# A graph layer's edge sum: the transposed node table built in the prologue, and another split of the gathers between engines

## The chip, the cores and the metric

The kernel runs on 1 core of a Trainium2 chip. The metric is the device time of one execution in microseconds (us); the time before is the median of three runs.

## The reference

One message-passing layer over a graph with 12500 nodes of 48 features and 400000 edges that are sorted by their destination. A node's features are normalised and rectified; for each edge, a two-layer perceptron takes destination, source and the edge's own 32 features; the messages are summed by destination and added to the input.

```python
h = jnp.maximum(_layernorm(x, axis=-1), 0.0)
x_i = h[dst]; x_j = h[src]
tmp = jnp.concatenate([x_i, x_j, edge_attr], axis=1)      # 48 + 48 + 32
h2 = jax.nn.relu(tmp @ W1 + b1)                           # 128 wide
msg = h2 @ W2 + b2                                        # 48 wide
out = x + jax.ops.segment_sum(msg, dst, num_segments=12500)
```

## The kernel before

`tmp @ W1` is split into three products. Two of them depend on a node alone, so a prologue (`node_tables`) makes two tables in DRAM: `tab_a` (what a node contributes as destination, with the bias) and `tab_b` (what it contributes as source), a row of 128 floats a node. The prologue goes over the nodes in six slices: VectorE and ScalarE normalise, PE transposes a slice into `ht`, and `table` multiplies it with the weights, two groups of 128 nodes a matmul; ScalarE and VectorE copy PSUM into `tab`, SyncE writes it out. First all of `tab_b`, then all of `tab_a`.

The main part (`windows`) goes over the 400000 edges in 391 chunks of 8 tiles of 128 edges. The 80 nodes from a chunk's first destination on are its window. Per chunk:

- `prepare`: SyncE loads the window's 80 rows of `tab_a` (`rhs`), the edges' features into the lower rows of `lhs`, and the destinations (`row`). VectorE compares `row` with the window's numbers, which makes a one-hot matrix in the upper rows of `lhs` and the nodes' degrees (`deg`), and makes a second one-hot matrix `hot`, with the edges along the partitions.
- `before`: PE multiplies `lhs` and `rhs` into `pre` (PSUM): destination and edge part of the hidden layer.
- `hidden`: VectorE adds the source part `gb`, ScalarE rectifies: `hid`.
- `fold`, `add`: PE sums `hid` by window node through `hot` into `p_g`; VectorE adds it into the running accumulator `seg` at the place of the window. Every 12 chunks a group's accumulator goes through W2 and out (`segment_*`).

The source part, a row of `tab_b` for each edge, comes in one of three ways:

- *gathers*: POOL issues one indirect DMA for a tile of 128 edges into `gb`. There are six `gb` buffers of a chunk each, so POOL runs up to six chunks ahead, until `hid` has read the oldest.
- *columns*: the transposed `tab_b` also lies in SBUF, as `bt` (128 x 12544). VectorE and ScalarE copy one column of four bytes per partition for an edge into a tile `gt`; a PE matmul (`turned` in `windows`) adds it into `pre`. The node's number is loaded from `last` into a register of the copying engine (`load`, by `numbers`), up to 32 a load instruction.
- *rows*: SyncE issues a DMA of one row for an edge into a tile `gs`, with the number from a register.

104 columns (44 on VectorE, 60 on ScalarE) and 12 rows are made per chunk, whatever tile they belong to; `BYCOLS` and `BYROWS` list the chunks whose last tile is complete by then and is not gathered. `PARTS` gives each part's engine, first column, size, and place in `last`.

`bt` is made in the first 13 chunks: `turn_load` reads 1024 rows of `tab_b` back from DRAM, `turn` transposes them with eight PE transposes, ScalarE copies them out. Columns therefore begin with chunk 14.

The order on each engine is that of the program text (a manual schedule). An iteration c of the main loop is written as follows, where each engine takes its own part in this order:

```python
prepare(c); turn_load(c); rows(c)
columns(c, 0); columns(c, 1)               # VectorE
before(c - 1); fold(c - 2); turned(c - 1)  # PE
columns(c, 2); hidden(c - 1)
load(c, 3); columns(c, 3)                  # ScalarE
add(c - 2)
load(c + 1, 0); load(c + 1, 2); turn(c)
```

`load(c, 1)` stands in `prepare`, between VectorE's comparison and `hot`. `deg` and `seg` are cleared at the head of `windows`, in a pool that takes the SBUF space the prologue's tiles give back.

Of the kernel before, what the change touches and what calls it, by code (L numbers as in the profile page):

```python
# [8 lines left out]
F32 = mybir.dt.float32  # L9
I32 = mybir.dt.int32  # L10
AF = mybir.ActivationFunctionType
ALU = mybir.AluOpType
# [18 lines left out]
L = 1024  # L31
# [14 lines left out]

BUILD = (NPAD + CE - 1) // CE
COLS = BUILD + 1  # L50
ROWS0 = 3
END = NT // T

PARTS = ((True, 0, 27, 1), (True, 27, 17, 28), (False, 44, 28, 48), (False, 72, 32, 76))
PART = sum(n for _, _, n, _ in PARTS)
BASE = 108
RPART = 12

BT0 = 16512


SEG, NEXT, SEG2 = 122, 123, 124
WIDTH = 128
SLOTS = (NCH + 2 + P - 1) // P
MOST = 32

# [15 lines left out]
GNACC = 4  # L82


def node_tables(nc, tc, keep, x, ident, w1, b1, tab_a, tab_b, loads, most, check, rest):

    slices = [(0, 8), (8, 16), (24, 20), (44, 20), (64, 20), (84, 14)]
    ns = len(slices)
# [3 lines left out]
    with ExitStack() as es:  # L92
# [72 lines left out]
        def table(j, wt, tv, dve):  # L165
# [17 lines left out]
                    nc.scalar.copy(to, of)  # L183
            nc.sync.dma_start(tv[:, r0 : r0 + rb, :], t)

        for i in range(ns + 3):
            if i < ns:
                centre(i)
            if 0 <= i - 1 < ns:
                scale(i - 1)  # L190
            if 0 <= i - 2 < ns:
                turn(i - 2)
            if i == ns + 1:
                most()
            if i == ns + 2:
                check()
            if 0 <= i - 3 < ns:
                table(i - 3, wb, tb_v, i >= ns)
        for j in range(ns):
            table(j, wa, ta_v, True)  # L200
        rest()


def windows(nc, tc, gp, bt, ident, idx, x_t, tab_a, tab_b, dst, edge_t, w1, w2s, b2s, out_t):


    srci, rel, bw, wrow, last = idx
    with ExitStack() as es:
        one = es.enter_context(tc.tile_pool(name="wone", bufs=1))
        ld = es.enter_context(tc.tile_pool(name="ld", bufs=3))  # L210
        gtp = es.enter_context(tc.tile_pool(name="gtp", bufs=3))
# [13 lines left out]
        for _, _, n, at in PARTS:  # L225
# [4 lines left out]
        rows_at = slice(BASE + 1, BASE + 1 + RPART)  # L230
# [3 lines left out]
        tab8 = tab_b.rearrange("n h -> (n h)").bitcast(U8)  # L234

        place = PARTS[0][3] - 1
        for a, b in ((place, SEG2), (NEXT, SEG)):
# [5 lines left out]
        segs = []  # L243
        for k in range(2):
            seg = one.tile([P, 2, L], F32, name=f"seg{k}")
            nc.vector.memset(seg, 0.0)
            segs.append(seg)
        degs = []
        for k in range(3):
            deg = one.tile([W, P], F32, name=f"deg{k}")  # L250
            nc.gpsimd.memset(deg, 0.0)
            degs.append(deg)

        rhss = []
        for k in range(3):
# [7 lines left out]
        def group(c):  # L263

            return divmod(c + OFF, GQ)
# [15 lines left out]
        def node(n):  # L281
            return n.with_bounds(min_val=0, max_val=N - 1)
# [11 lines left out]
                    tab8[bass.ds(n, 4 * HID)].rearrange("(o h) -> o h", o=1),  # L294
                )

        def turn_load(i):

            n = min(T, NR - i * T)
            t = wp.tile([P, T, HID], F32, name="hid")  # L300
            nc.sync.dma_start(
                t[:, :n, :],
                tab_b[i * CE : i * CE + n * P, :].rearrange("(t p) h -> p t h", p=P),
            )
            return n, t

        def turn(i, n, t):
            p_t = ps_p.tile([P, T, HID], F32, name="pre")
            for q in range(n):
                nc.tensor.transpose(p_t[:, q, :], t[:, q, :], ident)  # L310
            nc.scalar.copy(  # L311
                bt[:, i * CE : i * CE + n * P], p_t[:, :n, :].rearrange("h t p -> h (t p)")
            )

        regs = {}

        def load(c, part):

            dve, first, n, at = PARTS[part]
            n = max(0, min(n, len(BYCOLS) * P - ((c - COLS) * PART + first))) if c >= COLS else 0  # L320
            engine = mybir.EngineType.DVE if dve else mybir.EngineType.Activation
            if part == 0 and 2 <= c < NCH + 2:
                base, *nodes = numbers(c, at - 1, n + 1, engine)
                st[c - 2]["base"] = base.with_bounds(min_val=0, max_val=FAR)
            else:
                nodes = numbers(c, at, n, engine) if n else []
            regs[c, part] = nodes

        def columns(c, part):

            dve, first, _, _ = PARTS[part]
            copy = nc.vector.tensor_copy if dve else nc.scalar.copy
            for k, at in enumerate(regs.pop((c, part), [])):
                j, e = divmod((c - COLS) * PART + first + k, P)
                of = BYCOLS[j]
                if of not in gts:
                    gts[of] = gtp.tile([HID, P], F32, name="gt")
                at = at.with_bounds(min_val=BT0, max_val=BT0 + 4 * (N - 1)) - BT0
                copy(gts[of].bitcast(U8)[:, 4 * e : 4 * e + 4], bt8[:, bass.ds(at, 4)])  # L339

        def prepare(c):
            n = min(T, NT - c * T)
            at = c * CE
            m = max(0, min(RPART, len(BYROWS) * P - (c - ROWS0) * RPART)) if c >= ROWS0 else 0
            base, *nodes = numbers(c, BASE, 1 + m, mybir.EngineType.SP)
            rhs = rhss[c % 3]
            nc.sync.dma_start(rhs[:W, :], tab_a[bass.ds(node(base), W), :])
            lhs = ld.tile([P, CE], F32, name="lhs")
            nc.sync.dma_start(lhs[W:K, : n * P], edge_t[:, at : at + n * P])
            row = ld.tile([W, CE], I16, name="row")  # L350
            nc.sync.dma_start(
                row[:, : n * P],
                dst[at : at + n * P].rearrange("(o e) -> o e", o=1).to_broadcast([W, n * P]),
            )
            st[c] = dict(n=n, rows=nodes)
            gb = gp.tile([P, T, HID], F32, name="gb")
            for t in range(n - (c in BYCOLS) - (c in BYROWS)):
                nc.gpsimd.indirect_dma_start(  # L358
                    out=gb[:, t, :], out_offset=None, in_=tab_b[:, :],
                    in_offset=bass.IndirectOffsetOnAxis(  # L360
                        ap=srci[:, c * T + t : c * T + t + 1], axis=0
                    ),
                )

            deg = degs[c % 3]
            nc.vector.tensor_scalar(  # L366
                lhs[:W, : n * P], row[:, : n * P], bw[:, c : c + 1], None,
                op0=ALU.is_equal, op1=ALU.add, accum_out=deg[:, :1],
            )
            load(c, 1)  # L370
            hot = wp.tile([P, T, W], F32, name="hot")
            nc.vector.tensor_tensor(  # L372
                hot[:, :n, :], wnum.unsqueeze(1).to_broadcast([P, n, W]),
                rel[:, c * T : c * T + n].unsqueeze(2).to_broadcast([P, n, W]), op=ALU.is_equal,
            )
            st[c].update(rhs=rhs, lhs=lhs, gb=gb, deg=deg, hot=hot)

        def before(c):
# [43 lines left out]
        def add(c):  # L422

            s = st.pop(c)
            to = segs[group(c)[0] % 2][:, :, bass.ds(s["base"], W)]
            nc.vector.tensor_add(to, to, s["p_g"])  # L426

        xs = {}
# [31 lines left out]
        with tc.manual_schedule():  # L460
            for c in range(NCH + 2):
                if c < NCH:
                    prepare(c)
                    if c < BUILD:
                        part = turn_load(c)
                    rows(c, st[c].pop("rows"))
                columns(c, 0)
# [29 lines left out]
                if c < BUILD:  # L497
# [131 lines left out]
def tile_gnn_preln(  # L629
# [51 lines left out]
    bw = const.tile([W, NCH], F32, name="bw")  # L681
    flag = const.tile([1, 1], I32, name="flag")
    last = const.tile([P, SLOTS, WIDTH], I32, name="last")
    gp = ctx.enter_context(tc.tile_pool(name="gp", bufs=6))

    with tc.tile_pool(name="keep", bufs=1) as keep, tc.tile_pool(
# [68 lines left out]

        dsts = keep.tile([P, NT], F32, name="dsts")
        b0f = keep.tile([P, NCH], F32, name="b0f")
        node_tables(nc, tc, keep, x, ident, w1, b1, tab_a, tab_b, loads, most, check, rest)
    outside = nc.values_load(flag[:1, :1], min_val=0, max_val=1)

    with tc.If(outside == 0) as cmp:
        windows(nc, tc, gp, bt, ident, (srci, rel, bw, wrow, last), x_t, tab_a, tab_b, dst16, edge_t,
                w1, w2s, b2s, out_t)
    with cmp.Else():
        general(nc, tc, bt, ident, x_t, tab_a, tab_b, src_it, dst_it, dst, edge_t, w1, w2s, b2s,
# [71 lines left out]
```

## Time and profile before

| what | value |
|---|---|
| three runs | 4942.31, 4946.85, 4949.29 us; median 4946.85 |
| profiled execution | 4948.09 us, its span 4946.4 us |
| first gather on POOL | 67.24 us |
| `seg` of the first chunk, `seg` of the 15th | 147.3 us, 324.4 us |
| POOL's gathers (L358) | 2784 |
| column copies (L339) on ScalarE, VectorE | 22500, 16540 |
| row transfers (L292) | 4608 |
| register loads (L274) on VectorE | 800, median 1410 ns |
| granted TensorE clock, mean | 0.607 |

The times of the trace count from the span's start. An engine counts as busy while it carries out an instruction of its own; register loads, semaphore waits and the issue of a DMA don't count, and "issue" stands for idle time in which the profile shows nothing that the engine waited for. "remote" stands for a wait whose releaser isn't among the instructions shown.

### The profile page before, as it was taken

How to read it: one execution, taken by the hardware profiler on the slowest of the kernel's cores; microseconds unless marked ns; L12 is line 12 of the kernel's file. 1: busy time of each engine (PE TensorE's matmuls, PEld its weight loads, DVE VectorE, ACT ScalarE, POOL GpSimd, SP SyncE). 2: the span in 40 equal slices, each digit the busy share in tenths (PEclk: the TensorE clock that was granted, in tenths of full speed). 3: DMA queues.
4: the chain of work that ended last, by engine and by line, in shares of the span. 5: the costliest groups of instructions: out<-in, count | busy, mean ns of one | idle time of the engine just before them, and what ended most of it. 6: DMA issues, size and time to landing. Idle time of an engine off the chain costs nothing. (4 is left out here: it accounts for less than half of the span.)

```text
span 4946.4 us, 92158 instructions
## 1 busy us (share of the span) xinstructions
PE 3197.2 (65%) x14504; PEld 2884.0 (58%) x14504; DVE 2942.6 (59%) x18764; ACT 2864.2 (58%) x23270; POOL 2675.9 (54%) x2812
## 2 busy tenths in 40 slices
PE   4565666666666666666666666666666666666666
PEld 3555556555555555656555555655666555555656
DVE  3255666666666666566666666666566666666665
ACT  2146666666566666566656566666566666566665
POOL 5555555555555555555555555555555555555552
PEclk7665655566666565556565666555555665666555
DMA  5422222222222222222222222222222222222221
GB/s 208 111 78 71 70 70 67 68 70 72 70 70 68 67 70 71 70 70 69 66 70 71 70 70 68 67 70 70 70 70 68 68 69 71 70 69 69 70 67 51
DMA packets 214695, 363.63 MB, mean 74 GB/s; under 512 B 70419, under 2 KB 119717, under 8 KB 212805
## 3 DMA queue, kind: packets, MB, share of 16 engines
q0 software_dynamic: 89120, 182.66, 14.4%
q1 hardware_dynamic: 124704, 174.89, 11.8%
q14 instruction: 491, 4.01, 0.3%
q8 instruction: 120, 1.97, 0.2%
q10 hardware_dynamic: 260, 0.10, 0.0%
HBM read 337.91 MB, written 22.07 MB: 73 GB/s over the span
## 5 line engine op out<-in xcount | busy, mean ns | idle before, releaser
L358 POOL DMA_INDIRECT gb<-tab_b,srci x2784 | 2654.2, 953 | 2167.6 <-DVE seg L426 1273.1
L339 ACT COPY gt<-bt 128x4 uint8 x22500 | 2421.0, 189 | 1761.1 <-issue 1734.7
L339 DVE COPY gt<-bt 128x4 uint8 x16540 | 1516.0, 193 | 1464.2 <-issue 1457.9
L416 PE MATMUL p_g<-hot,hid 128*128 128x80 f32 x6250 | 1368.2, 407 | 1557.6 <-ACT hid L408 1446.3
L416 PEld LDWEIGHTS p_g<-hot,hid 128*128 128x128 f32 x6250 | 1291.5, 314 | 1648.2 <-ACT hid L408 1528.5
L384 PEld LDWEIGHTS pre<-rhs,lhs 112*128 112x128 f32 x6250 | 1254.8, 306 | 140.1 <-issue 95.7
L384 PE MATMUL pre<-rhs,lhs 112*128 112x128 f32 x6250 | 1291.4, 393 | 52.1 <-DVE hid L403 38.8
L366 DVE TENSOR_SCALAR_CACHE_REDUCE lhs<-row,bw 80x1024 f32<-80x1024 int16 x391 | 498.1, 1274 | 253.5 <-issue 181.1
L403 DVE TENSOR_TENSOR hid<-pre,gb 128x896 f32<-128x896 f32 (+2 forms) x391 | 429.7, 1099 | 67.5 <-remote 53.8
L408 ACT ACTIVATE hid<-hid 128x896 f32<-128x896 f32 (+1 forms) x391 | 376.1, 962 | 120.4 <-DVE hid L403 91.1
L372 DVE TENSOR_TENSOR hot<-wnum,rel 128x640 f32<-128x640 f32 x391 | 322.0, 823 | 95.7 <-issue 95.7
L394 PE MATMUL pre<-ident,gt 128*128 128x128 f32 x610 | 220.0, 464 | 93.6 <-remote 49.8
L419 PE MATMUL p_g<-ident,deg 80*128 80x80 f32 x782 | 237.4, 405 | 2.7 <-issue 2.7
L394 PEld LDWEIGHTS pre<-ident,gt 128*128 128x128 f32 x610 | 164.0, 328 | 101.3 <-remote 53.6
L419 PEld LDWEIGHTS p_g<-ident,deg 80*128 80x128 f32 x782 | 203.4, 317 | 2.7 <-issue 2.7
L426 DVE TENSOR_TENSOR seg<-seg,p_g 128x160 f32 x391 | 120.9, 309 | 51.3 <-issue 23.4
L452 PE MATMUL p_f<-seg,w2s 128*48 128x512 f32 (+1 forms) x134 | 121.9, 1010 | 0.4 <-DVE seg L426 0.4
L407 ACT ACTIVATE hid<-pre 128x128 f32<-128x128 f32 x305 | 81.9, 268 | 60.8 <-DVE hid L403 51.7
L453 PE MATMUL p_f<-seg,b2s 1*48 1x512 f32 (+1 forms) x134 | 111.2, 924 | 0.0
L453 PEld LDWEIGHTS p_f<-seg,b2s 1*48 1x48 f32 x134 | 14.5, 159 | 102.0 <-issue 102.0
L311 ACT COPY bt<-pre 128x1024 f32<-128x1024 f32 (+1 forms) x13 | 12.4, 957 | 94.7 <-remote 71.5
L454 DVE TENSOR_TENSOR xseg<-xseg,p_f 48x512 f32<-48x512 f32 (+1 forms) x67 | 45.0, 671 | 29.7 <-PE p_f L453 22.5
(65 smaller groups left out, 348.7 us busy)
## 6 DMA issues: line engine op xcount, KB each, us to landing
gs<-tab_b SPq DMA_DIRECT2D x4608, 0.5 KB
row<-in_dst SPq DMA_DIRECT2D x390, 160.0 KB
lhs<-in_edge_t SPq DMA_DIRECT2D x390, 128.0 KB
gb<-tab_b,srci POOLq DMA_INDIRECT x2784
rhs<-tab_a SPq DMA_DIRECT2D x391, 40.0 KB
xseg<-in_x_t SPq DMA_DIRECT2D x33, 192.0 KB
out_x<-xseg SPq DMA_DIRECT2D x33, 192.0 KB
hid<-tab_b SPq DMA_DIRECT2D x12, 512.0 KB
```

The costliest lines, as they stand in the source:

```text
L339: copy(gts[of].bitcast(U8)[:, 4 * e : 4 * e + 4], bt8[:, bass.ds(at, 4)])
L358: nc.gpsimd.indirect_dma_start(out=gb[:, t, :], out_offset=None, in_=tab_b[:, :], in_offset=bass.IndirectOffsetOnAxis(ap=srci[:, c * T + t ...
L366: nc.vector.tensor_scalar(lhs[:W, : n * P], row[:, : n * P], bw[:, c : c + 1], None, op0=ALU.is_equal, op1=ALU.add, accum_out=deg[:, :1],)
L372: nc.vector.tensor_tensor(hot[:, :n, :], wnum.unsqueeze(1).to_broadcast([P, n, W]), rel[:, c * T : c * T + n].unsqueeze(2).to_broadcast([P ...
L384: nc.tensor.matmul(pre[:, t, :], s["lhs"][:K, t * P : (t + 1) * P], s["rhs"][:K, :], start=True, stop=c not in BYCOLS or t < n - 1,)
L394: nc.tensor.matmul(s["pre"][:, s["n"] - 1, :], gts.pop(c), ident, start=False, stop=True)
L403: nc.vector.tensor_add(h[:, :g, :], pre[:, :g, :], s["gb"][:, :g, :])
L408: nc.scalar.activation(h[:, :m, :], h[:, :m, :], AF.Relu)
L416: nc.tensor.matmul(p_g[:, 0, :], s["h"][:, t, :], s["hot"][:, t, :], start=t == 0, stop=t == n - 1)
L419: nc.tensor.matmul(p_g[:, 1, :], s["deg"], ident[:W, :W], start=True, stop=True)
L452: nc.tensor.matmul(p_f[:, :n], w2s, seg[:, 0, s], start=True, stop=False)
L453: nc.tensor.matmul(p_f[:, :n], b2s[:1, :], seg[:1, 1, s], start=False, stop=True)
```

## The change

1. `bt` is made in the prologue. A new step `turned` (in `node_tables`) multiplies the same `ht` slices with the weights the other way round, so that PE's output is already transposed, 14 groups of up to four pairs of node columns, two matmuls each of up to 512 columns; ScalarE copies the even nodes, VectorE the odd ones into `bt`. It stands after `tab_b` and before `tab_a`. `turn_load` and `turn` go, and columns begin with chunk 1 (`COLS`), rows as well (`ROWS0`).
2. The tiles `deg` are cleared by POOL at the kernel's head, in a pool of their own, and no longer wait for the prologue's space; the accumulators `seg` get a pool that stands first.
3. 54 columns on VectorE and 60 on ScalarE, 14 rows: 128 edges a chunk. VectorE's columns come in three parts (24, 18, 12), each with a register load of its own: the first is loaded behind the previous `hid`, ahead of `add`; the second behind the comparison; the third behind `hot`. The first part's copies stand between the comparison and `hot`.
4. The places in `seg` and `tab_a` come from the table ready as byte addresses, so that VectorE's and SyncE's register arithmetic for them falls away, and a column copy is one float in place of four bytes.

```diff
-COLS = BUILD + 1
-ROWS0 = 3
+COLS = 1
+ROWS0 = 1
-PARTS = ((True, 0, 27, 1), (True, 27, 17, 28), (False, 44, 28, 48), (False, 72, 32, 76))
+PARTS = (
+    (True, 0, 24, 1), (True, 24, 18, 25), (True, 42, 12, 43),
+    (False, 54, 28, 56), (False, 82, 32, 84),
+)
-RPART = 12
+RPART = 14
...
+        def turned(j):
+
+            r0, rb = slices[j]
+            bt_v = bt.rearrange("h (p r) -> h p r", r=NR)
+            for g in range(0, rb // 2, 4):
+                n = min(4, rb // 2 - g)
+                for k in range(2):
+                    p_n = ps_n.tile([P, 2, 2 * HID], F32, name="p_n")
+                    of = p_n.rearrange("h a b -> h (a b)")[:, : n * P]
+                    nc.tensor.matmul(
+                        of, wb[:, k, :],
+                        hts[j][: 2 * D, g : g + n, :].rearrange("k q p -> k (q p)"),
+                        start=True, stop=True,
+                    )
+                    r = r0 + 2 * g + k
+                    to = bt_v[:, :, r : r + 2 * n - 1 : 2].rearrange("h p q -> h q p")
+                    of = of.rearrange("h (q p) -> h q p", p=P)
+                    if k:
+                        nc.vector.tensor_copy(to, of)
+                    else:
+                        nc.scalar.copy(to, of)
...
         for j in range(ns):
+            turned(j)
+        for j in range(ns):
             table(j, wa, ta_v, True)
...
-                at = at.with_bounds(min_val=BT0, max_val=BT0 + 4 * (N - 1)) - BT0
-                copy(gts[of].bitcast(U8)[:, 4 * e : 4 * e + 4], bt8[:, bass.ds(at, 4)])
+                copy(gts[of][:, e : e + 1], bt8[:, bass.ds(at, 4)].bitcast(F32))
...
             load(c, 1)
+            columns(c, 0)
             hot = wp.tile([P, T, W], F32, name="hot")
...
+            load(c, 2)
...
                 columns(c, 1)
+                columns(c, 2)
...
-                columns(c, 2)
+                columns(c, 3)
                 if 0 <= c - 1 < NCH:
                     hidden(c - 1)
-                load(c, 3)
-                columns(c, 3)
+                load(c + 1, 0)
+                load(c, 4)
+                columns(c, 4)
                 if 0 <= c - 2 < NCH:
                     add(c - 2)
...
-                load(c + 1, 0)
-                load(c + 1, 2)
+                load(c + 1, 3)
...
-                if c < BUILD:
-                    turn(c, *part)
...
+    degs = []
+    for k in range(3):
+        deg = const.tile([W, P], F32, name=f"deg{k}")
+        nc.gpsimd.memset(deg, 0.0)
+        degs.append(deg)
```

More of the change, by code (lines that the diff above doesn't have):

```diff
@@ L44 @@
 U8 = mybir.dt.uint8
-BUILD = (NPAD + CE - 1) // CE
-COLS = BUILD + 1
-ROWS0 = 3
+COLS = 1
+ROWS0 = 1
 END = NT // T
-PARTS = ((True, 0, 27, 1), (True, 27, 17, 28), (False, 44, 28, 48), (False, 72, 32, 76))
+PARTS = (
+    (True, 0, 24, 1), (True, 24, 18, 25), (True, 42, 12, 43),
+    (False, 54, 28, 56), (False, 82, 32, 84),
+)
 PART = sum(n for _, _, n, _ in PARTS)
-BASE = 108
-RPART = 12
+BASE = 116
+RPART = 14
 BT0 = 16512
-SEG, NEXT, SEG2 = 122, 123, 124
-WIDTH = 128
+SEG0 = 123360
+SEG_SIZE = 8 * L
+SEG, NEXT, SEG2 = 132, 133, 134
+PLACE0 = 135
+WIDTH = 136
 SLOTS = (NCH + 2 + P - 1) // P
@@ L82, with node_tables @@
 GNACC = 4
-def node_tables(nc, tc, keep, x, ident, w1, b1, tab_a, tab_b, loads, most, check, rest):
+def node_tables(nc, tc, keep, bt, x, ident, w1, b1, tab_a, tab_b, loads, most, check, rest):
     slices = [(0, 8), (8, 16), (24, 20), (44, 20), (64, 20), (84, 14)]
@@ L204, in windows @@
 def windows(nc, tc, gp, bt, ident, idx, x_t, tab_a, tab_b, dst, edge_t, w1, w2s, b2s, out_t):
-    srci, rel, bw, wrow, last = idx
+    srci, rel, bw, wrow, last, degs = idx
     with ExitStack() as es:
+        seg = es.enter_context(tc.tile_pool(name="segs", bufs=1))
+        segs = [seg.tile([P, 2, L], F32, name=f"seg{k}") for k in range(2)]
         one = es.enter_context(tc.tile_pool(name="wone", bufs=1))
@@ L229, in windows @@
             )
-        rows_at = slice(BASE + 1, BASE + 1 + RPART)
+        rows_at = slice(BASE, BASE + 1 + RPART)
         nc.vector.tensor_scalar(
@@ L233, in windows @@
         )
-        tab8 = tab_b.rearrange("n h -> (n h)").bitcast(U8)
+        tab8, taba8 = (t.rearrange("n h -> (n h)").bitcast(U8) for t in (tab_b, tab_a))
         place = PARTS[0][3] - 1
@@ L241, in windows @@
             )
-        segs = []
-        for k in range(2):
-            seg = one.tile([P, 2, L], F32, name=f"seg{k}")
-            nc.vector.memset(seg, 0.0)
[L247 to L252, printed above, removed]
+        at_place = slice(place, place + 1)
+        nc.vector.scalar_tensor_tensor(
+            last[:, :, at_place], last[:, :, at_place], 4.0, last[:, :, PLACE0 : PLACE0 + 1],
+            op0=ALU.mult, op1=ALU.add,
+        )
+        for seg in segs:
+            nc.vector.memset(seg, 0.0)
         rhss = []
@@ L295, in rows @@
                 )
[L297 to L313, printed above, removed]
         regs = {}
@@ L323, in load @@
                 base, *nodes = numbers(c, at - 1, n + 1, engine)
-                st[c - 2]["base"] = base.with_bounds(min_val=0, max_val=FAR)
+                st[c - 2]["base"] = base
             else:
@@ L337, in columns @@
                     gts[of] = gtp.tile([HID, P], F32, name="gt")
-                at = at.with_bounds(min_val=BT0, max_val=BT0 + 4 * (N - 1)) - BT0
-                copy(gts[of].bitcast(U8)[:, 4 * e : 4 * e + 4], bt8[:, bass.ds(at, 4)])
+                at = at.with_bounds(
+                    min_val=BT0, max_val=BT0 + 4 * (N - 1), guaranteed_mod_val=0, out_of_modulus=4
+                ) - BT0
+                copy(gts[of][:, e : e + 1], bt8[:, bass.ds(at, 4)].bitcast(F32))
         def prepare(c):
@@ L346, in prepare @@
             rhs = rhss[c % 3]
-            nc.sync.dma_start(rhs[:W, :], tab_a[bass.ds(node(base), W), :])
+            base = base.with_bounds(min_val=0, max_val=4 * HID * (N - 1))
+            nc.sync.dma_start(
+                rhs.bitcast(U8)[:W, :],
+                taba8[bass.ds(base, 4 * HID * W)].rearrange("(w h) -> w h", w=W),
+            )
             lhs = ld.tile([P, CE], F32, name="lhs")
@@ L424, in add @@
             s = st.pop(c)
-            to = segs[group(c)[0] % 2][:, :, bass.ds(s["base"], W)]
+            k = group(c)[0] % 2
+            of = SEG0 + k * SEG_SIZE
+            at = s["base"].with_bounds(
+                min_val=of, max_val=of + 4 * FAR, guaranteed_mod_val=0, out_of_modulus=4
+            ) - of
+            to = segs[k].bitcast(U8)[:, :, bass.ds(at, 4 * W)].bitcast(F32)
             nc.vector.tensor_add(to, to, s["p_g"])
@@ L463, in windows @@
                     prepare(c)
-                    if c < BUILD:
-                        part = turn_load(c)
                     rows(c, st[c].pop("rows"))
-                columns(c, 0)
+                if c >= NCH:
+                    columns(c, 0)
                 columns(c, 1)
+                columns(c, 2)
                 if 0 <= c - 1 < NCH:
@@ L496, in windows @@
                     segment_store(g, END_L)
-                if c < BUILD:
-                    turn(c, *part)
                 if c < PIECES:
@@ L757, in tile_gnn_preln @@
         b0f = keep.tile([P, NCH], F32, name="b0f")
-        node_tables(nc, tc, keep, x, ident, w1, b1, tab_a, tab_b, loads, most, check, rest)
+        node_tables(nc, tc, keep, bt, x, ident, w1, b1, tab_a, tab_b, loads, most, check, rest)
     outside = nc.values_load(flag[:1, :1], min_val=0, max_val=1)
     with tc.If(outside == 0) as cmp:
-        windows(nc, tc, gp, bt, ident, (srci, rel, bw, wrow, last), x_t, tab_a, tab_b, dst16, edge_t,
+        windows(nc, tc, gp, bt, ident, (srci, rel, bw, wrow, last, degs), x_t, tab_a, tab_b, dst16, edge_t,
                 w1, w2s, b2s, out_t)
@@ L790 @@
     numbers[2 : NCH + 2, SEG2] = seg
+    numbers[2 : NCH + 2, PLACE0] = SEG0 + of % 2 * SEG_SIZE
     numbers[:NCH, BASE] = first
```

## The prediction

> **What bounds the kernel now.** I read the page's groups first, then the waits, then the timelines of VectorE and of POOL through two chunks, last the timeline of the start. The page:
>
> ```profile
> PE 3197.2 (65%) x14504; PEld 2884.0 (58%) x14504; DVE 2942.6 (59%) x18764; ACT 2864.2 (58%) x23270; POOL 2675.9 (54%) x2812
> ...
> L358 POOL DMA_INDIRECT gb<-tab_b,srci x2784 | 2654.2, 953 | 2167.6 <-DVE seg L426 1273.1
> L339 ACT COPY gt<-bt 128x4 uint8 x22500 | 2421.0, 189 | 1761.1 <-issue 1734.7
> L339 DVE COPY gt<-bt 128x4 uint8 x16540 | 1516.0, 193 | 1464.2 <-issue 1457.9
> ```
>
> No engine is busy over two thirds, POOL waits on VectorE, and both column copiers lose over 1400 us to "issue", that is, to nothing the profile shows. The timeline of VectorE through one chunk (start, busy us, what, count, idle before) tells when:
>
> ```profile
> 2005.64 1.09 DVE L403 TENSOR_TENSOR hid<-pre,gb 128x896 f32<-128x896 f32 x1
> 2006.64 0.31 DVE L426 TENSOR_TENSOR seg<-seg,p_g 128x160 f32 x1
> 2007.46 1.27 DVE L366 TENSOR_SCALAR_CACHE_REDUCE lhs<-row,bw 80x1024 f32<-80x1024 int16 x1 [0.51 <-issue]
> ...
> 2009.01 0.82 DVE L372 TENSOR_TENSOR hot<-wnum,rel 128x640 f32<-128x640 f32 x1 [0.26 <-issue]
> 2009.75 1.96 DVE L339 COPY gt<-bt 128x4 uint8 x25
> 2011.91 0.17 DVE L339 COPY gt<-bt 128x4 uint8 x1 [0.20 <-issue]
> 2012.63 0.32 DVE L339 COPY gt<-bt 128x4 uint8 x2 [0.54 <-issue]
> 2014.05 0.24 DVE L339 COPY gt<-bt 128x4 uint8 x2 [1.10 <-issue]
> 2015.48 0.24 DVE L339 COPY gt<-bt 128x4 uint8 x2 [1.19 <-issue]
> 2016.90 0.95 DVE L339 COPY gt<-bt 128x4 uint8 x12 [1.17 <-issue]
> 2017.76 1.08 DVE L403 TENSOR_TENSOR hid<-pre,gb 128x896 f32<-128x896 f32 x1
> ```
>
> 25 copies go at 0.07 us each, then for 5.4 us only 7 get through, on a grid of 0.71 us, then 12 more at full pace, and hid follows at once. ScalarE's timeline has the same grid (single copies at 2011.91, 2012.63, 2013.35 and so on to 2016.89), and SyncE's row transfers are stretched as well (12 in 8.64 us, 5.00 us in a chunk where they fell differently). POOL beside it:
>
> ```profile
> 2007.00 0.94 POOL L358 DMA_INDIRECT gb<-tab_b,srci  x1 [3.79 <-DVE seg L426]
> ...
> 2014.49 0.95 POOL L358 DMA_INDIRECT gb<-tab_b,srci  x1 [0.30 <-issue]
> 2019.11 0.95 POOL L358 DMA_INDIRECT gb<-tab_b,srci  x1 [3.67 <-DVE hid L405]
> ...
> 2032.49 0.95 POOL L358 DMA_INDIRECT gb<-tab_b,srci  x1 [3.67 <-DVE seg L426]
> ```
>
> POOL issues a chunk's gathers 1.25 us apart, and the slow stretch of the others begins some 4.5 us after the first and ends about 1.45 us after the last. Then comes what VectorE has left of its columns, then hid, which frees a gather buffer (six of them), and POOL starts again 1.35 us after hid's start. So a chunk is a loop through two engines: gathers, tail, **VectorE's columns left over**, hid. With 7 gathers: 9.90 us from 2007.00 to the end of the slow stretch, 0.86 for the 12 copies (0.0717 each), 1.35: 12.11. With 8 (2019.11 to 2032.49): 13.38, 1.27 more. What the slow stretch is I can't tell from the profile; I take only its place from it.
>
> **The change, part by part.** The profiled execution took 4948 us (span 4946.4 and 2 around it); the median of three runs is 4947, so they agree.
>
> *Gathers.* 116 of 128 edges of a tile now leave POOL per chunk, then 128 of 128: counting tiles, 346 made of columns and 42 of rows in place of 305 and 36, so 2737 gathers in place of 2784. 47 x 1.25 = **-59 us**; nearly every chunk then has 7.
>
> *VectorE's columns, 44 to 54.* The order becomes: load of 25 numbers, seg, lhs, load of 18, 24 copies, hot, load of 12, 30 copies, hid. Before the slow stretch VectorE did hot and 25 copies; now it has the 24 copies and hot in the same time, since the copies begin where hot stood and hot's 0.82 comes out of the same stretch. 7 go in the stretch as now. 54 - 25 - 7 = 22 are left after it, 10 more: 0.72 us a chunk, on the path. Bounds: below, the 0.51 and 0.26 us of idle time before lhs and hot vanish too (-0.05 in all); above, the third load stands open, 1.41 us (median of VectorE's loads in the trace), 2.13 in all. I take it as hidden, since the 24 copies and hot in front of it are 2.5 us. If that cover is gone it costs up to 1.41 a chunk.
>
> *Register arithmetic.* One fused register operation a chunk leaves VectorE (0.07 us, behind hid) and one leaves SyncE (0.04). I count -0.07 for the first, nothing for the second: SyncE runs a chunk ahead. Copies of one float in place of four bytes: no row has that shape; between 0 and three element times, which the copies' spacing doesn't resolve. I take 0.
>
> So 0.65 us a chunk for the 376 chunks that had columns before: **+244 us**.
>
> *SyncE's rows, 12 to 14.* Two more transfers at 0.42 us (12 in 5.00) to 1.43 (two grid steps). SyncE goes from its first transfer of one chunk at 2007.17 to that of the next at 2018.73, 11.56 us; with the two at 0.42 it is 12.4, within the 12.76 that a chunk would take. I take 0; the hiding work is VectorE's longer chunk. ScalarE keeps its 60 copies and gains slack.
>
> *The start.* Away go 13 loads of 512 KB, 98 matmuls (18.3 us) and 13 copies on ScalarE (12.4 us) of the transposed table. Added are 28 matmuls with 12544 columns in all; table a's have 49 x 256 and took 21.3 us, so about 21 us on PE in the prologue, with 28 copies of up to 128x512 at 0.59 (ScalarE) to 0.69 us (VectorE) behind it. That pushes the end of the prologue, 66 us, to 87. Against this POOL need no longer wait for table a:
>
> ```profile
> 66.25 0.48 POOL L251 MEMSET deg<- 80x128 f32 x3 [35.52 <-ACT tab L183]
> 67.24 0.97 POOL L358 DMA_INDIRECT gb<-tab_b,srci  x1 [0.50 <-issue]
> ```
>
> Its first gather needs table b alone, whose last write is issued at 45.7; so POOL starts near 49 and does 47 gathers (six chunks) until 108. But a long run of gathers slows all: now VectorE's hid of the first chunk waits until deep in it:
>
> ```profile
> 124.30 1.22 DVE L403 TENSOR_TENSOR hid<-pre,gb 128x1024 f32<-128x1024 f32 x1 [35.15 <-remote]
> ```
>
> though PE's matmuls for it were over at 88.9. PE then advances one instruction per 0.7 us. From 53 to 110 that is some 80 of the 308 matmul and weight-load records that the two tables need, so the prologue would end near 131 and seg of the first chunk near 155, where it is at 147.3 now. Bounds: no slowing at all, seg near 112 (-35); a tail as long as the present one, 9 us after the last gather, and two slow chunks, +28. I take **+8**, by the rows of the first burst, which are nearest.
>
> Sum: 4948 - 59 + 244 + 8 = 5141, so **5140 us**.
>
> On the copies' new type, the Trainium skill speaks against the change: "SBUF — State Buffer", section "SBUF: two separate sides", says that an fp32 SBUF-to-SBUF copy on VectorE in a two-port mode locks POOL out of writing descriptors. By that rule some 32 copies a chunk, at their spacing, would hold POOL 2.3 us, and the estimate would be near 6000. But "VectorE: DVE Perf Modes", section "Mode 2×_2P — use both read ports for one tensor", splits the outermost dimension in half, and one element has no half. The trace has no such copy; with byte copies beside them and without (100 to 124 us) the gathers last 0.94 to 0.95 us alike.
>
> **Rivals.** *The copies fit (faster).* If the copies that now start ahead of hot, the loads in parts and the missing register operation let VectorE place the 10 more before the slow stretch, nothing is left over that isn't now: 4948 - 59 - 26 (0.07 x 376), with the start at -35 to +28, 4830 to 4890, near 4865. For it: 0.77 us of idle time stands before lhs and hot, as much as the 10 copies take. Against: that idle time is load time, and the loads stay. It decides at few copies: 59 us is paid for by 59 / (376 x 0.0717) = 2.2 exposed copies a chunk. *A draw.* 2 or 3 copies exposed, 4940 to 4960. *SyncE becomes the bound.* If one added row falls on the grid and one doesn't, its chunk is 11.56 + 1.85 = 13.4 us, 1.3 over now: 4948 - 59 + 490 = 5380. For it: between last row and next load it has almost no idle time now. Against: in the chunk with 8 gathers its rows took 5.00 us, so it has slack.
>
> **How the numbers follow.** The likeliest case, 10 copies exposed, gets 0.60, with its own range of 5015 (half of them fit) to 5250 (0.3 us of the third load open). The copies fit: 0.30. Draw: 0.05. SyncE: 0.05. A measurement of this kernel tells about 0.2% from no change, 10 us. So faster 0.31, same 0.04, slower 0.65. The range has to reach into the faster case: 4850 to 5240 leaves out about 2 in 10.
>
> **What would show it.** VectorE's copies after the slow stretch: about 22 in a row right ahead of hid (12 now); a spacing of POOL's first gathers of 12.8 us with 7 gathers. For the start: POOL's first gather near 49 us, PE's table matmuls spread out behind it, seg of the first chunk near 155. It is wrong if the run ahead of hid stays near 12, if the slow stretch gets shorter or ends earlier against the last gather, or if SyncE's next first transfer comes later than hid.

## The result and the profile after

The changed kernel takes 5235.27 us (median of four runs, 5232.24 to 5236.9) against 4945.22 for the kernel before (four runs): 1.0585 times as long, 95% interval 1.0567 to 1.0604. Its profiled execution has a span of 5233.9 us. 5140 was forecast, in a range of 4850 to 5240, whose upper end is 5 us away. The page's chain that ended last (DVE is VectorE, DVEq its sequencer, here its register loads), and its groups:

```profile
issue 17%; DVE 16%; DVEq 4%; PE 1%; ACT 0%; SPq 0%; ACTq 0%; another core or an unknown queue 0%; DMA 0%
...
L374 POOL DMA_INDIRECT gb<-tab_b,srci x2737 | 2595.8, 948 | 2533.5 <-DVE hid L421 1583.0
L351 ACT COPY gt<-bt 128x1 f32 x23282 | 2441.0, 187 | 1944.6 <-issue 1924.5
...
L351 DVE COPY gt<-bt 128x1 f32 x21006 | 1417.7, 145 | 1815.8 <-issue 1794.0
```

POOL has 47 gathers fewer and idles 366 us longer, most of it on hid. VectorE's 21006 copies are busy for less time than its 16540 were before, yet 352 us more of idle time stand before them, nearly all "issue". The timeline of VectorE through one chunk (start, busy us, what, count, idle before) shows where:

```profile
2008.62 1.08 DVE L421 TENSOR_TENSOR hid<-pre,gb 128x896 f32<-128x896 f32 x1
2010.41 0.32 DVE L449 TENSOR_TENSOR seg<-seg,p_g 128x160 f32 x1 [0.71 <-DVE hid L421]
2010.64 1.27 DVE L382 TENSOR_SCALAR_CACHE_REDUCE lhs<-row,bw 80x1024 f32<-80x1024 int16 x1
...
2014.84 1.55 DVE L351 COPY gt<-bt 128x1 f32 x24 [2.92 <-issue]
2017.04 0.82 DVE L389 TENSOR_TENSOR hot<-wnum,rel 128x640 f32<-128x640 f32 x1 [0.65 <-issue]
2018.65 0.21 DVE L351 COPY gt<-bt 128x1 f32 x2 [0.79 <-issue]
2019.15 0.15 DVE L351 COPY gt<-bt 128x1 f32 x1 [0.29 <-issue]
2019.86 1.73 DVE L351 COPY gt<-bt 128x1 f32 x27 [0.55 <-issue]
2021.50 1.08 DVE L421 TENSOR_TENSOR hid<-pre,gb 128x896 f32<-128x896 f32 x1
```

The 24 copies wait 2.92 us behind lhs, hot and the other copies come late, and 27 copies are left in a row ahead of hid (12 before, 22 forecast). Over all chunks with 7 gathers the median is 26, counting the copies that start after the slow stretch and before hid; before it was 12. POOL's first gathers of this chunk and the next stand 12.88 us apart, with 7 gathers, where 12.8 was forecast:

```profile
2009.97 0.95 POOL L374 DMA_INDIRECT gb<-tab_b,srci  x1 [4.51 <-DVE hid L421]
2022.85 0.95 POOL L374 DMA_INDIRECT gb<-tab_b,srci  x1 [4.43 <-DVE hid L421]
```

What fills the 2.92 us is VectorE's register loads. The answer on their line, for the 12.88 us of this chunk and then for a chunk of the kernel before (durations in ns: shortest, median, longest):

```profile
L302 DVEq TENSOR_LOAD <-last x3: 1894/2807/4160, 2008.4 to 2015.8; - x3
```

```profile
L274 DVEq TENSOR_LOAD <-last x2: 1398/1653/1908, 2005.4 to 2007.5; - x2
```

Before, 28 numbers took 1908 ns and 17 took 1398. Now 25 take 1894, but 18 take 4160 and 12 take 2807. In the program's order the load of 18 stands ahead of the 24 copies. It starts at 2010.6 and takes 4.16 us, and the first copy starts behind it, at 2014.84.

### The profile page after: what moved, and what is told of

It is laid out like the page before. It is cut to its first block, busy times and chain, and to the rows that moved or that the text cites. A ratio compares the mean times of both kernels' runs of the same rounds, so it can differ in the third digit from the quotient of the medians.

```text
span 5233.9 us, 98859 instructions
## 1 busy us (share of the span) xinstructions
PE 3314.1 (63%) x14544; PEld 2975.5 (57%) x14544; DVE 2881.0 (55%) x23252; ACT 2920.8 (56%) x24094; POOL 2617.5 (50%) x2765
## 5 line engine op out<-in xcount | busy, mean ns | idle before, releaser
L374 POOL DMA_INDIRECT gb<-tab_b,srci x2737 | 2595.8, 948 | 2533.5 <-DVE hid L421 1583.0
L351 ACT COPY gt<-bt 128x1 f32 x23282 | 2441.0, 187 | 1944.6 <-issue 1924.5
L434 PE MATMUL p_g<-hot,hid 128*128 128x80 f32 x6250 | 1409.7, 418 | 1763.2 <-ACT hid L426 1526.9
L351 DVE COPY gt<-bt 128x1 f32 x21006 | 1417.7, 145 | 1815.8 <-issue 1794.0
L434 PEld LDWEIGHTS p_g<-hot,hid 128*128 128x128 f32 x6250 | 1327.9, 323 | 1857.5 <-ACT hid L426 1610.7
L402 PEld LDWEIGHTS pre<-rhs,lhs 112*128 112x128 f32 x6250 | 1283.9, 313 | 109.1 <-issue 89.9
L402 PE MATMUL pre<-rhs,lhs 112*128 112x128 f32 x6250 | 1315.7, 399 | 17.5 <-DMA lhs<-in_edge_t 15.8
L382 DVE TENSOR_SCALAR_CACHE_REDUCE lhs<-row,bw 80x1024 f32<-80x1024 int16 x391 | 495.7, 1268 | 12.2 <-DMA row<-in_dst 7.6
L421 DVE TENSOR_TENSOR hid<-pre,gb 128x896 f32<-128x896 f32 (+1 forms) x391 | 422.3, 1080 | 0.2
L412 PE MATMUL pre<-ident,gt 128*128 128x128 f32 x692 | 249.5, 464 | 86.1 <-remote 75.0
L412 PEld LDWEIGHTS pre<-ident,gt 128*128 128x128 f32 x692 | 187.2, 330 | 92.9 <-remote 80.8
L465 DVE MEMSET seg<- 128x944 f32 x64 | 54.1, 845 | 9.6 <-issue 0.6
```

The lines of the kernel that those rows point to most:

```text
L351: copy(gts[of][:, e : e + 1], bt8[:, bass.ds(at, 4)].bitcast(F32))
L374: nc.gpsimd.indirect_dma_start(out=gb[:, t, :], out_offset=None, in_=tab_b[:, :], in_offset=bass.IndirectOffsetOnAxis(ap=srci[:, c * T + t ...
L382: nc.vector.tensor_scalar(lhs[:W, : n * P], row[:, : n * P], bw[:, c : c + 1], None, op0=ALU.is_equal, op1=ALU.add, accum_out=deg[:, :1],)
L402: nc.tensor.matmul(pre[:, t, :], s["lhs"][:K, t * P : (t + 1) * P], s["rhs"][:K, :], start=True, stop=c not in BYCOLS or t < n - 1,)
L412: nc.tensor.matmul(s["pre"][:, s["n"] - 1, :], gts.pop(c), ident, start=False, stop=True)
L421: nc.vector.tensor_add(h[:, :g, :], pre[:, :g, :], s["gb"][:, :g, :])
```

## The experiments

The runs came in three groups, each on one chip. The kernel before took 5002 us beside e1 to e4, 5009 beside e5 to e8 and 4946 beside e9 to e12, so only ratios to it are compared; the changed kernel's is 1.0585. It was not run again beside e1 to e12, so a difference to it counts only where it is clear of both intervals, of about 0.002 to each side.

**e1 to e4: one part each.** e1 moves the places of the numbers:

```diff
-    (True, 0, 24, 1), (True, 24, 18, 25), (True, 42, 12, 43),
-    (False, 54, 28, 56), (False, 82, 32, 84),
+    (True, 0, 24, 1), (True, 24, 18, 28), (True, 42, 12, 48),
+    (False, 54, 28, 60), (False, 82, 32, 88),
...
-BASE = 116
+BASE = 120
...
-SEG, NEXT, SEG2 = 132, 133, 134
-PLACE0 = 135
-WIDTH = 136
+SEG, NEXT, SEG2 = 136, 137, 138
+PLACE0 = 139
+WIDTH = 140
```

> The changed kernel with one thing altered: each of VectorE's three groups of numbers starts at a place in `last` that is a multiple of four words (16 bytes): 0, 28, 48 in place of 0, 25, 43 (and ScalarE's and SyncE's at 60, 88, 120). Theory: in the changed kernel VectorE's load of 18 numbers takes 4.16 us and that of 12 takes 2.81, 0.23 a number, while before a load of 17 takes 1.40 and one of 28 takes 1.91, 0.23 for each four; what differs is that 25 and 43 are no multiples of four and 28 was one. Then here the load of 18 takes about 1.6 and that of 12 about 0.9 to 1.2, the 24 copies begin about 2.5 us earlier, hot lies ahead of the slow stretch, and 20 to 23 copies are left after it instead of 27: 5100 to 5160 us. Rival (the loads are long because of where they stand in the order, beside lhs and in the slow stretch): both durations stay, and the time stays at 5235.

1.0254 (1.0237 to 1.0271; 5130.5 us). The load lines of a chunk, two loads and then the third:

```profile
L302 DVEq TENSOR_LOAD <-last x2: 1604/1754/1903, 2009.2 to 2011.5; - x2
```

```profile
L302 DVEq TENSOR_LOAD <-last x1: 874/874/874, 2014.3 to 2014.3; - x1
```

The load of 18 went from 4160 to 1604 ns, that of 12 from 2807 to 874. VectorE's timeline between them and hid:

```profile
2013.19 1.69 DVE L351 COPY gt<-bt 128x1 f32 x24 [0.36 <-issue]
2014.80 0.81 DVE L389 TENSOR_TENSOR hot<-wnum,rel 128x640 f32<-128x640 f32 x1
2015.53 0.41 DVE L351 COPY gt<-bt 128x1 f32 x3
...
2020.77 1.36 DVE L351 COPY gt<-bt 128x1 f32 x21 [0.55 <-issue]
2022.05 1.08 DVE L421 TENSOR_TENSOR hid<-pre,gb 128x896 f32<-128x896 f32 x1
```

The idle time ahead of the 24 copies is 0.36 us in place of 2.92, hot and three more copies go at full pace, and 21 are left, the number that the prediction's step gave (22). The rival, that the order makes the loads long, falls: the order is the same. ScalarE's and SyncE's groups move as well, but from one multiple of four words to another. Beside the starts one thing changes: a register operation of 46 ns stands ahead of each seg again (391 in e1's trace and in those of e4 to e11, none in the changed kernel's), which works against the gain. 0.0331 of 4945 us, **164 us of the 290, were two starts that were no multiple of four words**, more than the 75 to 135 expected; 4 of it lie in the start, where the first seg came at 173.3 (177.3 in the changed kernel).

e2 does the reverse to the kernel before:

```diff
-PARTS = ((True, 0, 27, 1), (True, 27, 17, 28), (False, 44, 28, 48), (False, 72, 32, 76))
+PARTS = ((True, 0, 27, 1), (True, 27, 17, 29), (False, 44, 28, 48), (False, 72, 32, 76))
```

> The kernel before with one thing altered: VectorE's second group of 17 numbers starts at word 29 of `last` instead of 28. Theory of the starts: its load grows from 1.40 to 17 x 0.23, some 3.9 to 4.2 us; hot, which stands behind it, begins where the slow stretch begins, so that the 25 copies that went ahead of it are left over as well: 24 to 26 x 0.0717 more in a chunk, up to 5650 us, and not under 5300. Rival (order and number of loads are what counts, not the start): 4945 as before.

1.0258 (1.0241 to 1.0275; 5130.6 us). The load took what was expected, 3934 ns for 1398, and hot waited 2.80 us, but the time rose by 129 us, not by 350 or more. The timeline says why:

```profile
2007.43 1.09 DVE L403 TENSOR_TENSOR hid<-pre,gb 128x896 f32<-128x896 f32 x1
...
2013.34 0.82 DVE L372 TENSOR_TENSOR hot<-wnum,rel 128x640 f32<-128x640 f32 x1 [2.80 <-issue]
2014.08 2.09 DVE L339 COPY gt<-bt 128x4 uint8 x25
2017.34 0.17 DVE L339 COPY gt<-bt 128x4 uint8 x1 [1.18 <-issue]
2018.07 0.17 DVE L339 COPY gt<-bt 128x4 uint8 x1 [0.55 <-issue]
2018.77 1.31 DVE L339 COPY gt<-bt 128x4 uint8 x17 [0.53 <-issue]
```

25 copies go at full pace although they begin 6.6 us behind hid, where the kernel before had long slowed down (its slow copies began 6 us behind hid). So the slow stretch has no fixed start. Some 25 short instructions pass first, late as they come here, and only then does the grid begin (22 to 33 in most chunks of the runs; more in e8); it ends, as before, behind POOL's last gather. A late start costs only the few that the grid would have let through, here 17 left in place of 12: 5 x 0.0717 x 376 = 135 us, near the 129. Of my expectation the load's length came true, and what it costs did not.

e3 brings back byte copies:

```diff
-                copy(gts[of][:, e : e + 1], bt8[:, bass.ds(at, 4)].bitcast(F32))
+                copy(gts[of].bitcast(U8)[:, 4 * e : 4 * e + 4], bt8[:, bass.ds(at, 4)])
```

> The changed kernel with the column copies of VectorE and ScalarE as four bytes again in place of one float. If the float form is what brought VectorE's spacing from 0.072 to 0.061 us: 27 left over x 0.0107 x 376 = 108 more, 5340 us. If the spacing has another cause or the type doesn't matter: 5235.

1.0753 (1.0735 to 1.0771; 5379.3 us): 83 us more than the changed kernel, where 108 were expected. Its copies left over:

```profile
2018.77 1.95 DVE L351 COPY gt<-bt 128x4 uint8 x26 [0.54 <-issue]
```

25 spacings in 1.95 less one copy of 0.17 are 0.071 us each, against (1.73 - 0.145) / 26 = 0.061 in the changed kernel. The type sets the pace. POOL's gathers last 948 ns in the mean in both kernels.

e4 makes POOL wait for the prologue's end again:

```diff
-    degs = []
-    for k in range(3):
-        deg = const.tile([W, P], F32, name=f"deg{k}")
-        nc.gpsimd.memset(deg, 0.0)
-        degs.append(deg)
...
+        degs = []
+        for k in range(3):
+            deg = one.tile([W, P], F32, name=f"deg{k}")
+            nc.gpsimd.memset(deg, 0.0)
+            degs.append(deg)
```

> The changed kernel with the tiles deg cleared in `windows` as before, so that POOL's gathers wait for the prologue's end. If the gathers slow the prologue down and that is what moved the first seg to 177: the prologue ends at 85 to 95 instead of 133, the first gather is near 90, the first seg near 165 to 172, and the time 5222 to 5230. If the head start of the gathers outweighs the slowing: first seg near 190 to 200, time 5250 to 5260. In both the chunks of the loop stay at 12.9 us.

1.0555 (1.0537 to 1.0573; 5281.4 us), 15 us under the changed kernel, at the edge of what the intervals tell apart; the traces are clearer. First seg is at 169.9 us for 177.3, the first gather at 92.4, and the prologue ends at 91. Busy times by stretch (from and to, length, PE, PE's loads, VectorE, ScalarE, POOL, granted clock, DMA), first of the changed kernel, then of e4:

```profile
52.00:69.00 17.00, 16.52 (x44) 7.37 (x42) 9.17 (x10) 9.75 (x10) 12.63 (x14) 1.00 0.18 47
69.00:107.00 38.00, 10.98 (x25) 6.45 (x24) 2.69 (x3) 2.05 (x3) 28.85 (x31) 0.55 0.24 68
107.00:134.00 27.00, 20.70 (x76) 16.30 (x75) 6.65 (x10) 7.03 (x12) 0.13 (x1) 0.76 0.44 181
```

```profile
44.00:92.00 48.00, 46.62 (x168) 30.76 (x166) 22.98 (x31) 23.71 (x31) 0.48 (x3) 1.00 0.38 157
92.00:152.00 60.00, 7.54 (x32) 6.97 (x32) 13.85 (x63) 2.79 (x28) 41.62 (x44) 0.51 0.42 123
```

Beside 31 gathers PE gets 25 matmuls done in 38 us and VectorE and ScalarE three copies each; without them 168 in 48 us. The head start was eaten at once: with all six buffers full, POOL stood still for 56.84 us:

```profile
106.19 0.94 POOL L374 DMA_INDIRECT gb<-tab_b,srci  x1 [0.30 <-issue]
163.97 0.94 POOL L374 DMA_INDIRECT gb<-tab_b,srci  x1 [56.84 <-DVE hid L421]
```

**e5 to e8: how many, and in what order.** All four stand on the changed kernel with starts at multiples of four. e5 has the split of before:

```diff
-    (True, 0, 24, 1), (True, 24, 18, 25), (True, 42, 12, 43),
-    (False, 54, 28, 56), (False, 82, 32, 84),
+    (True, 0, 24, 1), (True, 24, 8, 28), (True, 32, 12, 36),
+    (False, 44, 28, 48), (False, 72, 32, 76),
...
-BASE = 116
-RPART = 14
+BASE = 108
+RPART = 12
...
```

> The changed kernel with its groups of numbers at multiples of four words (as e1) and with the split of before: 44 columns on VectorE (24, 8, 12), 60 on ScalarE, 12 rows, so 2784 gathers or so. Theory (VectorE's columns left after the slow stretch set the chunk): 10 to 11 copies fewer are left than e1's 21, at 0.061 each 0.61 to 0.67 us a chunk less, and 0.12 more for the gathers: 0.96 to 1.00 times the kernel before on the same chip (e1 was 1.025). Rival (the new order and the third load cost, or another engine bounds): it stays above 1.01.

0.9915 (0.9898 to 0.9931; 4966.7 us). In chunks of 7 gathers the median of the copies left is 12, for 21 in e1; one such chunk:

```profile
2049.44 0.82 DVE L351 COPY gt<-bt 128x1 f32 x12 [0.56 <-issue]
2050.18 1.08 DVE L421 TENSOR_TENSOR hid<-pre,gb 128x896 f32<-128x896 f32 x1
```

The float copy alone gives the same ratio (e12, 0.9923). So with 44 columns the table in the prologue, the new order and its three loads together bring and cost nothing that is seen: the ten more columns do.

e6 takes more away (against e5):

```diff
-    (True, 0, 24, 1), (True, 24, 8, 28), (True, 32, 12, 36),
-    (False, 44, 28, 48), (False, 72, 32, 76),
+    (True, 0, 24, 1), (True, 24, 4, 28), (True, 28, 4, 32),
+    (False, 32, 20, 36), (False, 52, 32, 56),
...
-BASE = 108
+BASE = 88
...
```

> As e5 with fewer columns, 32 on VectorE (24, 4, 4), 52 on ScalarE, 12 rows: 96 edges a chunk, so 7.25 gathers in the mean. Theory: VectorE has nothing or nearly nothing left after the slow stretch, hid starts at its end, and a chunk of 7 gathers takes 11.4 to 11.5 us, one of 8 12.7 to 12.8; in the mean 11.8 to 12.0, so 0.94 to 0.97 times the kernel before. Rival (a gather is worth more than 1.25 us, or another engine bounds near 12): not under 1.00.

0.9703 (0.9687 to 0.972; 4859.8 us), at the theory's upper end. None or one copy is left in most chunks of 7, and such a chunk takes 11.55 us in the median, but one of 8 takes 13.0, not 12.8. Idle time now stands ahead of hid in place of copies:

```profile
L421 DVE TENSOR_TENSOR hid<-pre,gb 128x896 f32<-128x896 f32 (+2 forms) x391 | 437.9, 1120 | 825.4 <-issue 742.5 <-PE pre L412 62.4 <-PE pre L402 12.8
```

Most of it is "issue". hid starts 1.8 us behind the end of POOL's last gather in the median, so a chunk of 7 is its gathers, that tail and POOL's start again: 8.45 + 1.8 + 1.35 = 11.6 us.

e7 moves columns from VectorE to SyncE's rows (against e5):

```diff
-    (True, 0, 24, 1), (True, 24, 8, 28), (True, 32, 12, 36),
-    (False, 44, 28, 48), (False, 72, 32, 76),
+    (True, 0, 24, 1), (True, 24, 8, 28), (True, 32, 4, 36),
+    (False, 36, 28, 40), (False, 64, 32, 68),
...
-BASE = 108
-RPART = 12
+BASE = 100
+RPART = 24
...
```

> As e5 with 36 columns on VectorE (24, 8, 4), 60 on ScalarE and 24 rows: 120 edges a chunk, 7.06 gathers in the mean. Theory, with SyncE off the path: 2 to 6 copies left, a chunk near 11.7 us, 0.94 to 0.97 times the kernel before. Rival (SyncE's rows bound, which the prediction's third rival said of 14 rows): 24 rows on the grid of 0.71 us make the chunk 14 us or more, over 1.08.

1.1495 (1.1476 to 1.1514; 5756.8 us): the theory was wrong and the rival right. Two lines of VectorE's groups and two of SyncE's timeline:

```profile
L351 DVE COPY gt<-bt 128x1 f32 x13968 | 923.9, 141 | 68.8 <-issue 66.8
L382 DVE TENSOR_SCALAR_CACHE_REDUCE lhs<-row,bw 80x1024 f32<-80x1024 int16 x391 | 498.1, 1274 | 2924.7 <-DMA row<-in_dst 2570.0 <-issue 323.9 <-DMA gs<-tab_b 30.9
```

```profile
2008.59 8.84 SPq L320 DMA_DIRECT2D gs<-tab_b  x24
...
2021.62 10.40 SPq L320 DMA_DIRECT2D gs<-tab_b  x24
```

lhs waits 2924.7 / 391 = 7.5 us a chunk, mostly for the transfer of `row`, which in the program's order SyncE issues behind the 24 rows of the chunk before. The copies hardly wait any more, because VectorE starts them late, when the gathers are over. The chunk is 14.4 us.

e8 has e5's split and this order on VectorE:

```diff
-            load(c, 1)
-            columns(c, 0)
             hot = wp.tile([P, T, W], F32, name="hot")
...
+            load(c, 0)
+            load(c, 1)
             load(c, 2)
...
                 if c >= NCH:
-                    columns(c, 0)
-                columns(c, 1)
-                columns(c, 2)
+                    load(c, 0)
...
                     hidden(c - 1)
-                load(c + 1, 0)
+                for k in range(3):
+                    columns(c, k)
```

> As e5 (44 columns, 60, 12 rows), but VectorE's order is: hid, all 44 copies, seg, lhs, hot, the three loads, hid, so that the copies come before the slow stretch and the large instructions and the loads lie in it. Theory (some 25 short instructions pass at full pace wherever they start, e2 showed that, and the rest one or two per 0.71 us): the copies start 3 us earlier than in e5, 4 to 8 fewer are left at the end of the stretch: a chunk 0.2 to 0.5 us shorter than e5's. Rival (the loads, which now lie ahead of hid, end after the slow stretch): a chunk 1 us or more longer than e5's.

1.0558 (1.0541 to 1.0576; 5286.8 us). This kernel delivers other sums, by an instruction that I did not find, so its time is not that of a usable version; its timeline still shows where VectorE's instructions lie:

```profile
3014.31 2.08 DVE L351 COPY gt<-bt 128x1 f32 x33
...
3021.14 0.32 DVE L449 TENSOR_TENSOR seg<-seg,p_g 128x160 f32 x1 [0.57 <-issue]
3021.84 1.27 DVE L382 TENSOR_SCALAR_CACHE_REDUCE lhs<-row,bw 80x1024 f32<-80x1024 int16 x1 [0.38 <-issue]
...
3025.67 1.09 DVE L421 TENSOR_TENSOR hid<-pre,gb 128x896 f32<-128x896 f32 x1 [1.59 <-PE pre L412]
```

The copies are over ahead of seg, where the theory had 4 to 8 left at the stretch's end, yet hid comes no earlier: seg and lhs are now late and hid waits for PE (508.7 us in all on L412). So a chunk lost nearly what the rival said (0.8 us over e5's in the mean, span against span over 391 chunks), by a wait that neither side had named. The copies start here with POOL's first gather (3014.31 and 3014.66), and more pass at full pace than elsewhere, 33 in this chunk and 30 to 44 in most. So a count of 25 alone does not tell where the grid begins.

**e9 to e12: what is worth keeping.** e9 is e6 with e4's edit. e10 and e11 are e9 with another split, first e10, then e11:

```diff
-    (True, 0, 24, 1), (True, 24, 4, 28), (True, 28, 4, 32),
-    (False, 32, 20, 36), (False, 52, 32, 56),
+    (True, 0, 20, 1), (True, 20, 4, 24), (True, 24, 4, 28),
+    (False, 28, 12, 32), (False, 40, 32, 44),
...
```

```diff
-    (True, 0, 24, 1), (True, 24, 4, 28), (True, 28, 4, 32),
-    (False, 32, 20, 36), (False, 52, 32, 56),
+    (True, 0, 24, 1), (True, 24, 8, 28), (True, 32, 4, 36),
+    (False, 36, 20, 40), (False, 56, 32, 60),
...
-RPART = 12
+RPART = 14
...
```

e12 is the kernel before with the float copy alone:

```diff
-                at = at.with_bounds(min_val=BT0, max_val=BT0 + 4 * (N - 1)) - BT0
-                copy(gts[of].bitcast(U8)[:, 4 * e : 4 * e + 4], bt8[:, bass.ds(at, 4)])
+                at = at.with_bounds(
+                    min_val=BT0, max_val=BT0 + 4 * (N - 1), guaranteed_mod_val=0, out_of_modulus=4
+                ) - BT0
+                copy(gts[of][:, e : e + 1], bt8[:, bass.ds(at, 4)].bitcast(F32))
```

> e6 (32 columns on VectorE, 52 on ScalarE, 12 rows, starts at multiples of four words; 0.970 of the kernel before) with e4's edit, POOL's gathers behind the prologue. Theory: the two gains add, 7 to 15 us below e6, so 0.967 to 0.969 of the kernel before on the same chip. Rival (with fewer columns the head start of the gathers is what counts): 0.971 or more.

> As e9 with 28 columns on VectorE (20, 4, 4) and 44 on ScalarE: 84 edges a chunk, 7.34 gathers in the mean. Theory: VectorE has nothing left to save after the stretch, so the added gathers (0.09 x 1.25 = 0.12 us a chunk, 46 us in all) count in full, less what PE's and ScalarE's waits ahead of hid give back: 0.968 to 0.980, not below e9. Rival (ScalarE's copies still bound): below e9 by 1% or more.

> As e9 with 36 columns on VectorE (24, 8, 4) and 14 rows: 102 edges a chunk, 7.20 gathers. Theory: some 4 copies more are left (0.24 us) against 0.06 us of gathers: 0.970 to 0.985, above e9. Rival (copies still fit): 0.960 to 0.966.

> The kernel before with the column copies as one float in place of four bytes, and nothing else. Theory: the spacing of VectorE's copies falls from 0.072 to 0.061 us here as well, and the 12 left over take 0.13 us less a chunk: 0.988 to 0.992 of the kernel before. Rival (the spacing belongs to the new order): 1.000.

| run | median us | ratio to before | 95% |
|---|---|---|---|
| e9 | 4795.5 | 0.9689 | 0.9672 to 0.9706 |
| e10 | 4879.6 | 0.9879 | 0.9857 to 0.9901 |
| e11 | 4833.7 | 0.9769 | 0.9752 to 0.9786 |
| e12 | 4908.8 | 0.9923 | 0.9906 to 0.9939 |

e9 has the lowest ratio, within its theory's range, but is not told apart from e6, so that the two gains add is not shown. e11 came as expected, and e12 lies at the upper end of its range. e10 missed: it is above its range of 0.968 to 0.980. By the ratios it lost 94 us to e9, twice the 46 of its added gathers, by the medians 84; but its four runs spread over 35 us, and the two profiled executions lie only 56 apart (4861.4 and 4805.0). What the rest is stays open. Of the splits tried, 32 and 52 is the best. e12's rest of copies, in the order of before:

```profile
2026.74 0.82 DVE L341 COPY gt<-bt 128x1 f32 x12 [0.54 <-issue]
2027.48 1.08 DVE L405 TENSOR_TENSOR hid<-pre,gb 128x896 f32<-128x896 f32 x1
```

12 copies in 0.82 us where they took 0.95.

## Why the prediction was right

- *VectorE's leftover copies set the chunk.* Right, and shown from both sides: 54, 44 and 32 columns (e1, e5, e6; 14 rows in e1 and 12 in the others, and 8 columns fewer on ScalarE in e6) left 21, 12 and none or one and gave 1.025, 0.992 and 0.970.
- *10 more copies left, 0.72 us.* Two sizes inside this term were off, in opposite directions. The load of 18 was taken to cost what the load of 17 had cost in its place, and the third was priced by the median of 1.41 us and taken as hidden; they took 4.16 and 2.81, for their starts, and their cover did not suffice: +164 us (e1). The pace was taken as unchanged, "between 0 and three element times"; it fell by 0.010 us a copy: -83 us (e3).
- *7 copies in the stretch as now.* Wrong in the changed kernel (3), nearly right once the loads are short (6 in e1's chunk above). The fixed start of the stretch, 4.5 us behind the first gather, was the wrong picture (e2); it cost the forecast little, because there too some 25 copies pass first.
- *The gathers.* 47 fewer, as counted; they still last 0.95 us and stand 1.25 apart.
- *SyncE's rows at 0.* Right for 14: in three chunks its rows took 5.50, 4.15 and 7.38 us, and lhs idles 12.2 us in all. The rival of SyncE has its place at 24 rows (e7).
- *The start, +8.* The parts up to the prologue's end were right: first gather 52.4 (49 forecast), 44 gathers until 107.1 (47 until 108), the prologue's last copy over at 133.3 (131). Wrong was the step from there to the first seg, 24 us, which took 44. SyncE's first chunk is issued only at 138.8 behind other loads, its row lands at 147, and three long register loads (5.39, 4.05 and 2.72 us) stand before the first hid: seg at 177.3, +30 in place of +8. e4 gives 7 us of it back, e1 4; the rest was not tried.
- *The sum.* 4 of e1's 164 us lie in the start's 22, so 5141 + 160 - 83 + 22 = 5240, against 5235; each of the two ratios is good to some 9 us. That the forecast was only 95 us low, and the measured time still inside the range, owes something to luck: two errors cancel by half.
- *The rival "the copies fit"* had named the right way to a gain, with the wrong number: they fit at 32, not at 54.

The Trainium skill's "SBUF — State Buffer", section "SBUF: two separate sides", which was weighed against the change, did not decide here: with float copies and with byte copies the gathers last 948 ns in the mean, and no run shows them held. On the loads, "Runtime: NRT & Kernel Launch", section "Instruction fetch mechanics", gives some 200 ns a register, even in bulk. That page speaks of loads from HBM, while `last` lies in SBUF. The loads from a start that is no multiple of four come near it (4160 / 18 = 231 ns); the others do not (1908 / 28 = 68), and there the measurement decides.

## What to carry to other kernels

Where a stretch of a loop slows every engine but one, count what an engine has left at its end: 10 columns saved 10/128 of a gather, 0.10 us, and left 9 copies more, 0.55 us (e1 against e5). Price a moved or added register load by its own count and start, not by a median over loads of another shape. A head start in a producer with six buffers was worth nothing here, where the consumer could not begin, and it slowed the consumer's preparation (e4).

## What the runs showed of the hardware that was not expected

- A register load's time depends on where its numbers start: from a multiple of four words (16 bytes) 12 numbers took 0.87 us, 25 took 1.90, 28 took 1.91, 17 took 1.40 and 18 took 1.60, about 0.09 and 0.26 for each whole four and each number over; from other starts 12 took 2.81, 17 took 3.93, 18 took 4.16 and 24, from word 1 in the first chunk, 5.39, about 0.23 for each one. All of these other starts are odd words; even ones that are no multiple of four were not tried.
- On VectorE a copy of one float per partition follows the one before it in 0.061 us, a copy of four bytes in 0.071 (changed kernel against e3, e12 against the kernel before).
- While POOL issues gathers, VectorE gets some 25 short instructions through at full pace (22 to 33 in most chunks, more in e8) and then one or two per 0.71 us, until about 1.5 us after the end of the last gather (1.45 in the changed kernel's chunk, 1.54 in e2's). What holds them is not settled by any of these runs.
